# Head softmax ordered over pairs of blocks, its inverse from Ln and Exp with a Newton step, expert gates and ups in separate banks, and layer-norm roots as powers on POOL

## The chip, the core and the metric

The kernel runs on one core of a Trainium2 chip. The core has a matrix engine (TensorE, PE in the profile; its weight loads are the row PEld), a vector engine (VectorE, DVE), an engine for activation functions (ScalarE, ACT), a general engine (GpSimd, POOL), and an engine that issues transfers (SyncE, SP). Each works through its own instructions in order and waits on the others through semaphores. ScalarE holds one set of function tables at a time; a change of set appears in the profile as an instruction of its own, ACT_TABLE_LOAD. The metric is the time of one execution in device microseconds (us), the median of several runs.

## What is computed

Two batches of 1024 tokens of 128 features, all in 32-bit floats, pass through eight residual blocks: x = x + f(layernorm(x)) for each f. The first layer has a latent attention, a spiking feed-forward, a state-space block and the spiking feed-forward again. The second layer has a linear attention, an expert feed-forward, a head attention and the expert feed-forward again. The parts that matter here are the layer norm, the state space's softplus, the head attention and the experts:

```python
def _layernorm(x, axis=-1, eps=1e-05):
    m = jnp.mean(x, axis=axis, keepdims=True)
    v = jnp.var(x, axis=axis, keepdims=True)
    return (x - m) / jnp.sqrt(v + eps)
...
    dp = jnp.einsum('bhqd,bhkd->bhqk', q, k) * SCALE      # 16 heads of 8 features
    attn = jax.nn.softmax(dp, axis=1)                     # over the heads, not the keys
    w_avg = jnp.einsum('bhqk,bhkd->bhqd', attn, v)
...
    def expert_step(acc, w):                              # 8 experts, summed for every token
        wg, wu, wd = w
        h = jax.nn.silu(x @ wg) * (x @ wu)
        return (acc + h @ wd, None)
```

The head attention's softmax runs over the 16 heads: for each pair of a query and a key, the 16 exponentials are divided by their sum. The delta of the state space is softplus(...), which the kernel works out with an Exp and an Ln.

## The kernel before

Tokens lie 128 to a tile, so there are 16 tiles, 8 to a batch. The first layer and the linear attention, with a part of the first expert feed-forward beside them, take the trace up to about 1068 us. Then heads_and_experts (L1128) does the head attention of both batches together with most of both expert feed-forwards, and experts_ffn (L924) does the last four tiles' experts.

**Layer norms.** StagedNorm (L49) takes mean and variance on DVE (stats), a square root on ACT (root, L66), a reciprocal on DVE (L69), and, where ACT is to apply the norm, a shift of -mean/deviation on DVE (L77). The state space's double norm (L655 to L666) works out two variances with six small DVE operations and takes both square roots on ACT.

**Head attention.** For each batch, each query tile and each key tile there is one block: 128 keys by 128 queries by 16 heads, 128 blocks in all. A block passes these steps, each on its engine:

- products (L1231): PE writes the scores of 16 heads into PSUM, four banks, of which there is one set (ps_s);
- maxima (L1248) and the subtraction (L1254), each over 128x2048, on DVE;
- exponentials (L1257) on ACT, two instructions of 128x1024;
- lower (L1262): SP copies the exponentials of heads 0 to 7 into a buffer for a pair of blocks; upper (L1265): POOL issues a transfer that adds those of heads 8 to 15;
- denominators (L1271): PE sums the eight parts and turns them in the same go, into a bank h_pd of its own (one buffer, ps_d), both blocks of the pair, first half of the heads (end of an even iteration), then the second half (odd iteration);
- inverse (L1283): DVE's reciprocal over both blocks; turned (L1288): PE turns it back; evacuated (L1292): ACT copies it out of PSUM;
- normalize (L1296): POOL multiplies a block's 128x2048 exponentials with the inverse;
- weigh (L1301): PE applies the values, 32 narrow matmuls.

**Experts beside them.** An expert unit is 256 tokens (a chunk), one of 8 experts and one of 4 slices of its hidden features: 320 units here. In ExpertStream.products (L1051) a unit takes one PSUM bank (e_pgu, two buffers): Wg's product in one half, Wu's in the other. gates (L1067) applies Silu to the first half on ACT, multiply (L1075) multiplies with the second on DVE, outputs (L1085) adds Wd's product to a sum. Up to two units are started in each iteration; where PE has a side step instead (turning a finished chunk, a step of a norm or of a preparation), one.

**Order.** The order of the stage is written out by hand (manual_schedule): one loop over i (L1374 and on), in which every engine gets its instructions in the order of the text. Iteration i makes the scores of block i+1, its maxima, subtraction and exponentials, the summing transfer of block i, normalizes block i-4 and weighs block i-5. Even and odd iterations differ in the denominators and in the inverse, which is made at the start of an even one. The function aside gives one step of a side list to an engine where it fits: openings of expert chunks (L1030: statistics, root, shift, application, turning) and preparations of the next batch (L1168). Before and after the loop, alone (L1340) runs the experts without heads.

## Time and profile before

| | |
|---|---|
| time, median of 3 runs | 2212.57 us (2206.4 to 2213.07) |
| the profiled execution | 2201.0 us, of which the span of the trace is 2199.3 us |
| PE busy | 1876.8 us, 85% |
| DVE busy | 1656.2 us, 75% |
| ACT busy | 1324.5 us, 60% |
| POOL busy | 870.1 us, 40% |
| first and last scores of the head stage | 1184.8 and 2039.0 us |
| table loads of the head stage's gates and exponentials | 134 and 128, 1283 ns each |
| granted TensorE clock, mean | 0.943 |

Busy shares are means over the whole span, and the stages differ: a share says little of what a stage waits for. In a line of a group the columns are the kernel's line, the engine, the operation, the tiles written and read, their shapes and the number of instructions; then the busy time in us and the mean in ns; then the idle time of the engine just before them and what ended it. In a line of the timeline the first number is the start in us from the start of the span, the second the time that the merged instructions took, and a bracket gives the idle time before and its releaser.

### The profile page before, as it was taken

To read this page: it belongs to the slowest core of one execution; us is meant where nothing else is said; L and a number is where in the kernel's file an instruction comes from. 1 tells how busy PE (TensorE), PEld (TensorE's weight loads), DVE (VectorE), ACT (ScalarE), POOL (GpSimd) and SP (SyncE) were. 2 spreads that over 40 slices of the span, in tenths; PEclk is the share of its full clock that TensorE was granted. 3 is DMA by queue.
4 is the path that set the end of the run, shared out by engine and by line. 5 is a ranking of instruction groups with operands and counts; after the bars stand their busy time and mean duration, and the time that the engine had idled before them with its cause. 6 is when DMAs were issued, how large, how long until landed. Compare 5 with 4: busy or idle time off the path is not lost. (4 is left out here: it accounts for less than half of the span.)

```text
span 2199.3 us, 33893 instructions
## 1 busy us (share of the span) xinstructions
PE 1876.8 (85%) x13632; PEld 1068.8 (49%) x13632; DVE 1656.2 (75%) x1955; ACT 1324.5 (60%) x1762; POOL 870.1 (40%) x432
## 2 busy tenths in 40 slices
PE   7669888889967758898688899999888999998999
PEld 4223243333334323334455566666566666666754
DVE  5976867898774699894424989889888989998422
ACT  1026512276633666763544888888888888888422
POOL 0013400063401000000100778777877878887600
PEclk9989979979988979999899999999999999999999
DMA  4000000197623287530001656665655666666200
GB/s 91 1 1 1 1 1 0 49 228 165 157 71 99 57 201 174 136 82 0 1 1 48 154 153 159 155 161 148 160 152 155 165 154 159 168 159 154 68 5 5
DMA packets 73789, 220.01 MB, mean 100 GB/s; under 512 B 9184, under 2 KB 19872, under 8 KB 73504
## 3 DMA queue, kind: packets, MB, share of 16 engines
q1 hardware_dynamic: 54736, 149.40, 23.3%
q0 software_dynamic: 18432, 67.12, 16.0%
q8 instruction: 107, 1.75, 0.3%
q10 hardware_dynamic: 464, 1.33, 0.3%
q14 instruction: 50, 0.41, 0.1%
HBM read 78.35 MB, written 5.24 MB: 38 GB/s over the span
## 5 line engine op out<-in xcount | busy, mean ns | idle before, releaser
L1296 POOL TENSOR_TENSOR h_e<-h_e,h_r 128x2048 f32<-128x2048 f32 x128 | 599.8, 4687 | 109.6 <-issue 100.0
L1248 DVE TENSOR_REDUCE h_m<-h_s 128x128 f32<-128x2048 f32 x128 | 292.7, 2287 | 71.4 <-PE h_s L1237 71.4
L1254 DVE TENSOR_TENSOR h_e<-h_s,h_m 128x2048 f32<-128x2048 f32 x128 | 293.2, 2290 | 9.6 <-DVE h_m L1248 0.4
L1257 ACT ACTIVATE h_e<-h_e 128x1024 f32<-128x1024 f32 x256 | 256.5, 1049 | 23.0 <-DVE h_e L1254 19.4
L1067 ACT ACT_TABLE_LOAD x134 | 171.9, 1283 | 71.6 <-PE e_pgu L1060 70.5
L385 POOL TENSOR_SCALAR_AFFINE_SELECT a_pT<-a_pT 128x256 f32<-128x256 f32 x120 | 128.5, 1092 | 203.2 <-ACT a_pT L382 200.5
L1060 PE MATMUL e_pgu<-e_uT,Wg 128*128 128x256 f32 x640 | 199.8, 395 | 4.4 <-ACT h_qz L1204 2.3
L1075 DVE TENSOR_TENSOR e_h<-e_sg,e_pgu 128x256 f32<-128x256 f32 x320 | 119.6, 402 | 107.7 <-ACT e_sg L1067 103.9
L287 DVE TENSOR_REDUCE a_nm<-a_s 128x2 f32<-128x1024 f32 (+7 forms) x144 | 167.9, 1217 | 38.3 <-PE a_s L278 26.8
L1060 PE MATMUL e_pgu<-e_uT,Wu 128*128 128x256 f32 x640 | 193.8, 385 | 0.0
L1237 PE MATMUL h_s<-h_qz,h_kT 32*128 32x512 f32 x1024 | 153.5, 668 | 46.0 <-DVE h_e L1254 43.2
L1085 PE MATMUL h_po<-e_h,Wd 128*128 128x256 f32 x640 | 188.7, 412 | 4.0 <-DVE e_h L1075 2.3
L1271 PE MATMUL h_pd<-ident,h_e 128*128 128x128 f32 x1024 | 144.9, 279 | 40.8 <-DMA h_e<-h_e 40.7
L1265 POOL DMA_DIRECT2D h_e<-h_e x128 | 119.5, 933 | 140.8 <-DVE h_m L1248 67.7
L382 ACT ACTIVATE a_pT<-a_st 128x1024 f32<-128x1024 f32 (+3 forms) x176 | 129.9, 791 | 65.4 <-PE a_st L368 62.6
L1067 ACT ACTIVATE e_sg<-e_pgu 128x256 f32<-128x256 f32 x320 | 111.5, 382 | 91.6 <-PE e_pgu L1060 76.3
L1257 ACT ACT_TABLE_LOAD x128 | 164.2, 1283 | 2.3
L1085 PEld LDWEIGHTS h_po<-e_h,Wd 128*128 128x128 f32 x640 | 112.8, 196 | 105.6 <-issue 78.9
L800 DVE TENSOR_TENSOR_SCAN s_h<-s_a,s_h 128x1024 f32<-128x1024 f32 x64 | 148.7, 2323 | 17.9 <-ACT s_a L768 14.1
L269 PE MATMUL a_s<-a_latT,a_qT 32*128 32x512 f32 (+3 forms) x768 | 117.0, 583 | 42.0 <-DVE a_nm L287 40.0
L1271 PEld LDWEIGHTS h_pd<-ident,h_e 128*128 128x128 f32 x1024 | 116.7, 142 | 66.7 <-DMA h_e<-h_e 47.0
L1301 PE MATMUL h_po<-h_e,h_vz 128*32 128x128 f32 x4096 | 138.4, 276 | 7.3 <-DVE x_res L1398 6.1
(293 smaller groups left out, 3118.2 us busy)
## 6 DMA issues: line engine op xcount, KB each, us to landing
h_e<-h_e SPq DMA_DIRECT2D x128, 512.0 KB, 4.6
h_e<-h_e POOLq DMA_DIRECT2D x128, 512.0 KB, 5.4
s_a<-s_steps SPq DMA_DIRECT2D x64, 512.0 KB, 5.1
s_h<-s_steps SPq DMA_DIRECT2D x64, 512.0 KB, 6.5
s_steps<-s_gate SPq DMA_DIRECT2D x8, 256.0 KB, 2.0
Wg<-in_Wg_dram SPq DMA_DIRECT2D x8, 256.0 KB, 5.9
Wu<-in_Wu_dram SPq DMA_DIRECT2D x8, 256.0 KB, 5.9
Wd<-in_Wd_dram SPq DMA_DIRECT2D x8, 256.0 KB, 6.0
```

The costliest lines, as they stand in the source:

```text
L287: nc.vector.tensor_reduce(nm[:, half, i, h : h + together], s[:, :, :n], AX.X, ALU.max, negate=True)
L800: nc.vector.tensor_tensor_scan(h, a, h, 0.0, ALU.mult, ALU.add)
L1060: nc.tensor.matmul(pgu[:, k, :], w[name][:, e, f], uT, start=True, stop=True)
L1067: nc.scalar.activation(sg, pgu[:, 0, :], AF.Silu)
L1085: nc.tensor.matmul(self.sums, self.w["Wd"][:, e, fc, :], h, start=False, stop=last, skip_group_check=True)
L1237: nc.tensor.matmul(s[:, j, :].rearrange("p (k q) -> p k q", k=K), kTs[b][quad, bass.ts(kb, P)], qzs[b][qb // 4][quad, :, bass.ts(qb % 4, P ...
L1248: nc.vector.tensor_reduce(m, heads.rearrange("p h q -> p q h"), AX.X, ALU.max)
L1254: nc.vector.tensor_sub(e, heads, m.unsqueeze(1).to_broadcast([P, H, P]))
L1257: nc.scalar.activation(eh, eh, AF.Exp, scale=scale)
L1271: nc.tensor.matmul(pd[:, t, :], pair[:, t, k, :], g.ident, start=(k == 0 and t == 0), stop=(k == 7), is_transpose=True, skip_group_check=True,
L1296: nc.gpsimd.tensor_mul(e, e, r.unsqueeze(1).to_broadcast([P, H, P]))
L1301: nc.tensor.matmul(po[32 * j : 32 * j + 32, :], vz[:, kb * J + j, k].rearrange("p a d -> p (a d)"), a[:, 4 * j + k, :], start=False, stop= ...
```

## The change

Four things change.

- **Norms.** root becomes two POOL operations, an addition of epsilon and a power of -0.5; the square roots on ACT and the reciprocals on DVE go. The state norm's chain of six DVE operations and a square root becomes three POOL operations. In the loop the side step of a root moves from ACT's place to POOL's.
- **The inverse of the denominators.** The reciprocal on DVE is replaced by exp(-ln(d)) on ACT (seed), and a Newton step of two operations on DVE (refined). The sign that the step leaves is turned in the copy on ACT (evacuated). A one-column Ln of a constant (log_and_exp) is put behind the gates of each odd iteration.
- **The order.** The denominators are summed block by block of a pair, not half by half: the first block at the end of an even iteration, the second near the start of the odd one, followed there by the seed. The refinement, the turning and the copy stay in the even iteration.
- **The experts.** An odd iteration makes the gate products of up to two pairs of units, a bank for a pair (rise), and their Silus over 512 columns (open_gates). The even iteration makes the Wu products of the same pairs in banks of their own (follow_up). The next odd iteration multiplies (multiply_pairs). PE's side steps take the place of one of the two banks of an odd iteration, or stand in an even one if fewer than two pairs are open. The preparations of the next batch now also wait until the chunks that they read have been added.

```diff
         make_identity(nc, self.ident)
-        self.eps = self.const.tile([P, 1], F32, name="eps")
-        nc.vector.memset(self.eps, EPS)
+        self.power = self.const.tile([P, 1], F32, name="power")
+        nc.vector.memset(self.power, -0.5)
...
     def root(self):
-        self.g.nc.scalar.activation(self.rs, self.mv[:, :, 1], AF.Sqrt, bias=self.g.eps)
-
-    def inverse(self):
-        self.g.nc.vector.reciprocal(self.rs, self.rs)
-
-    def inverse_and_shift(self):
-
-
-        self.inverse()
-        self.shift = self.g.small.tile([P, self.nt], F32, name=f"{self.key}_nb", bufs=2)
+        g = self.g
+        g.nc.gpsimd.tensor_scalar(self.rs, self.mv[:, :, 1], EPS, None, ALU.add)
+        g.nc.gpsimd.tensor_tensor(self.rs, self.rs, g.power.to_broadcast([P, self.nt]), ALU.pow)
+
+    def shift(self):
+
+        self.nb = self.g.small.tile([P, self.nt], F32, name=f"{self.key}_nb", bufs=2)
         for t in range(self.nt):
             self.g.nc.vector.tensor_scalar(
-                self.shift[:, t : t + 1], self.mv[:, t, 0:1], self.rs[:, t : t + 1], -1.0, ALU.mult, ALU.mult
+                self.nb[:, t : t + 1], self.mv[:, t, 0:1], self.rs[:, t : t + 1], -1.0, ALU.mult, ALU.mult
             )
...
             self.g.nc.scalar.activation(
-                dst[:, t, :], self.src[:, t, :], AF.Identity, bias=self.shift[:, t : t + 1], scale=self.rs[:, t : t + 1]
+                dst[:, t, :], self.src[:, t, :], AF.Identity, bias=self.nb[:, t : t + 1], scale=self.rs[:, t : t + 1]
             )
...
         rs = g.small.tile([P, 2, 4], F32, name="s_rs", bufs=2)
-        nc.vector.tensor_scalar(rs[:, 0, :], mv[:, :, 1], EPS, None, ALU.add)
-        nc.vector.reciprocal(rs[:, 0, :], rs[:, 0, :])
-        nc.vector.tensor_mul(rs[:, 1, :], rs[:, 0, :], mv[:, :, 1])
-        nc.vector.tensor_scalar(rs[:, 1, :], rs[:, 1, :], EPS, None, ALU.add)
-        nc.vector.reciprocal(rs[:, 1, :], rs[:, 1, :])
-        nc.vector.tensor_mul(rs[:, 1, :], rs[:, 1, :], rs[:, 0, :])
-        nc.scalar.activation(rs, rs, AF.Sqrt)
+        nc.gpsimd.tensor_scalar(rs[:, 1, :], mv[:, :, 1], 1.0 + EPS, EPS * EPS, ALU.mult, ALU.add)
+        nc.gpsimd.tensor_scalar(rs[:, 0, :], mv[:, :, 1], EPS, None, ALU.add)
+        rf = rs.rearrange("p a b -> p (a b)")
+        nc.gpsimd.tensor_tensor(rf, rf, g.power.to_broadcast([P, 8]), ALU.pow)
         yield
...
         self.g, self.w, self.work, self.ps, self.sums, self.zero = g, w, work, ps, sums, zero
+        self.risen, self.opened, self.paired, self.added = [], [], [], set()
         self.units, self.fresh, self.gated, self.ready, self.summed, self.done = [], [], [], [], [], []
...
         yield "dve", lambda: ln.stats(range(2))
-        yield "act", ln.root
-        yield "dve", ln.inverse_and_shift
+        yield "pool", ln.root
+        yield "dve", ln.shift
         yield "act", lambda: ln.apply_on_act(u)
...
         nc = self.g.nc
-        for chunk, e, fc, pgu in self.fresh:
-            sg = self.work.tile([P, 2 * P], F32, name="e_sg", bufs=4)
-            nc.scalar.activation(sg, pgu[:, 0, :], AF.Silu)
-            self.gated.append((chunk, e, fc, pgu, sg))
+        if self.fresh:
+            two = self.work.tile([P, 2, 2 * P], F32, name="e_sg2")
+            for k, (chunk, e, fc, pgu) in enumerate(self.fresh):
+                nc.scalar.activation(two[:, k, :], pgu[:, 0, :], AF.Silu)
+                self.gated.append((chunk, e, fc, pgu, two[:, k, :]))
         self.fresh = []
...
         nc = self.g.nc
-        for chunk, e, fc, pgu, sg in self.gated:
-            h = self.work.tile([P, 2 * P], F32, name="e_h", bufs=4)
-            nc.vector.tensor_mul(h, sg, pgu[:, 1, :])
-            self.ready.append((chunk, e, fc, h))
+        if self.gated:
+            two = self.work.tile([P, 2, 2 * P], F32, name="e_h2")
+            for k, (chunk, e, fc, pgu, sg) in enumerate(self.gated):
+                nc.vector.tensor_mul(two[:, k, :], sg, pgu[:, 1, :])
+                self.ready.append((chunk, e, fc, two[:, k, :]))
         self.gated = []
+
+    def rise(self, banks):
+
+        for _ in range(banks):
+            pair, self.units = self.units[:2], self.units[2:]
+            if pair:
+                self.risen.append((pair, self.halves("Wg", pair)))
+
+    def halves(self, name, pair):
+        pgu = self.ps.tile([P, 4, P], F32, name="e_pgu").rearrange("p (k a) b -> p k (a b)", k=2)
+        for k, (chunk, e, fc, uT) in enumerate(pair):
+            self.g.nc.tensor.matmul(pgu[:, k, :], self.w[name][:, e, bass.ts(fc, P)], uT, start=True, stop=True)
+        return pgu
+
+    def open_gates(self):
+        for pair, pgu in self.risen:
+            sg = self.work.tile([P, 2, 2 * P], F32, name="e_sg2")
+            self.g.nc.scalar.activation(sg[:, : len(pair)], pgu[:, : len(pair)], AF.Silu)
+            self.opened.append((pair, sg))
+        self.risen = []
+
+    def follow_up(self):
+        self.paired += [(pair, sg, self.halves("Wu", pair)) for pair, sg in self.opened]
+        self.opened = []
+
+    def multiply_pairs(self):
+        for pair, sg, pgu in self.paired:
+            h = self.work.tile([P, 2, 2 * P], F32, name="e_h2")
+            self.g.nc.vector.tensor_mul(h[:, : len(pair)], sg[:, : len(pair)], pgu[:, : len(pair)])
+            self.ready += [(chunk, e, fc, h[:, k, :]) for k, (chunk, e, fc, uT) in enumerate(pair)]
+        self.paired = []
...
             self.turned = None
+            self.added.add(chunk)
             xt = self.tokens(chunk)
...
         nc.vector.memset(zero, 0.0)
+        ones = one.tile([P, 1], F32, name="h_ones")
+        nc.vector.memset(ones, 1.0)
+        spare = one.tile([P, 1], F32, name="h_spare")
         held = ps_o.tile([P, 4 * P], F32, name="h_po")
...
                 yield "dve", lambda t=t: ln.stats((t, t + 1))
-            yield "act", ln.root
-            yield "dve", ln.inverse_and_shift
+            yield "pool", ln.root
+            yield "dve", ln.shift
             yield "act", lambda: ln.apply_on_act(u)
...
-        def denominators(pd, pair, half):
-
-            for k in range(4 * half, 4 * half + 4):
-                for t in range(2):
-                    nc.tensor.matmul(
-                        pd[:, t, :],
-                        pair[:, t, k, :],
-                        g.ident,
-                        start=(k == 0 and t == 0),
-                        stop=(k == 7),
-                        is_transpose=True,
-                        skip_group_check=True,
-                    )
-
-        def inverse(pd):
-            rT = work.tile([P, 2, P], F32, name="h_rT")
-            nc.vector.reciprocal(rT, pd[:, 0:2, :])
+        def denominators(pd, pair, t):
+
+            for k in range(8):
+                nc.tensor.matmul(
+                    pd[:, t, :],
+                    pair[:, t, k, :],
+                    g.ident,
+                    start=(t == 0 and k == 0),
+                    stop=(k == 7),
+                    is_transpose=True,
+                    skip_group_check=True,
+                )
+
+        def seed(pd):
+            rT = work.tile([P, 2, P], F32, name="h_rT", bufs=1)
+            nc.scalar.activation(rT, pd[:, 0:2, :], AF.Ln)
+            nc.scalar.activation(rT, rT, AF.Exp, scale=-1.0)
             return rT
+
+        def refined(pd, rT):
+
+            t = work.tile([P, 2, P], F32, name="h_t", bufs=1)
+            nc.vector.tensor_mul(t, rT, pd[:, 0:2, :])
+            nc.vector.scalar_tensor_tensor(rT, t, 2.0, rT, ALU.subtract, ALU.mult)
...
             r = work.tile([P, 2, P], F32, name="h_r")
-            nc.scalar.copy(r, pd[:, 2:4, :])
+            nc.scalar.mul(r, pd[:, 2:4, :], -1.0)
             return r
+
+        def log_and_exp():
+            nc.scalar.activation(spare, ones, AF.Ln)
...
-        side = [(0, 28 if k else 16, ex.opening(c)) for k, c in enumerate(first[1:])]
-        side += [(0, 64, preparation(1, 0))]
-        side += [(2 * c + 2, 16 if c else 28, ex.opening(c)) for c in second]
-        side.insert(len(first) + 1, (0, 24, preparation(1, 1)))
+        side = [(0, 28 if k else 16, ex.opening(c), ()) for k, c in enumerate(first[1:])]
+        side += [(0, 64, preparation(1, 0), first[:2])]
+        side += [(2 * c + 2, 16 if c else 28, ex.opening(c), ()) for c in second]
+        side.insert(len(first) + 1, (0, 24, preparation(1, 1), first[2:]))
         finished, current, head, ex.unopened = 0, None, None, len(first)
...
                         if not side or side[0][0] > finished or len(ex.units) > side[0][1]:
+                            return False
+                        if not ex.added.issuperset(side[0][3]):
                             return False
...
             spread(0)
-            e_, pairs, d_, r_ = {}, {}, {}, {}
+            e_, pairs, d_, r_, s_ = {}, {}, {}, {}, {}
...
                 now, resting, oT = resting, oT, None
+                even = i % 2 == 0
                 if i + 1 < n:
                     heads = products(*blocks[i + 1])
-                even = i % 2 == 0
-                due = even and 0 <= i - 4 < n
-                if due:
-                    rT = inverse(d_[i - 4])
+                if not even:
+                    ex.multiply_pairs()
+                pair = i - 4 if even else i - 3
+                due = 0 <= pair < n
+                if due and even:
+                    refined(d_[pair], s_[pair])
+                    turned(d_[pair], s_.pop(pair))
+                    r_[pair] = evacuated(d_.pop(pair))
+                elif due:
+                    denominators(d_[pair], pairs.pop(pair), 1)
+                    s_[pair] = seed(d_[pair])
                 if now is not None:
...
                     ex.outputs()
-                ex.multiply()
-                if due:
-                    turned(d_[i - 4], rT)
-                    r_[i - 4] = evacuated(d_.pop(i - 4))
-                ex.products(1 if ex.turn() or aside("pe") else 2)
+                if not even:
+                    ex.rise(1 if ex.turn() or aside("pe") else 2)
+                else:
+                    if len(ex.opened) < 2 and not ex.turn():
+                        aside("pe")
+                    ex.follow_up()
                 if resting is not None:
...
                 aside("act")
-                ex.gates()
+                if not even:
+                    ex.open_gates()
+                    log_and_exp()
                 if i + 1 < n:
...
                 aside("dve")
-                pair = i - 2 if even else i - 3
-                if not even and 0 <= pair < n:
-                    denominators(d_[pair], pairs.pop(pair), 1)
                 if 0 <= i - 4 < n:
...
                 aside("pool")
+                if even and 0 <= i - 2 < n:
+                    d_[i - 2] = ps_d.tile([P, 4, P], F32, name="h_pd")
+                    denominators(d_[i - 2], pairs[i - 2], 0)
                 if 0 <= i - 5 < n:
...
-                if even and 0 <= pair < n:
-                    d_[pair] = ps_d.tile([P, 4, P], F32, name="h_pd")
-                    denominators(d_[pair], pairs[pair], 0)
+            ex.follow_up()
+            ex.multiply_pairs()
             while ex.busy() or side or current:
```

Left out are the places where inverse and inverse_and_shift are called in the first layer: the former call is dropped, the latter becomes shift.

More of the change, by code (lines that the diff above doesn't have):

```diff
@@ L232, in project @@
                 ln.root()
-                ln.inverse()
                 ln.apply(u, range(4), nc.vector)
@@ L541, in spiking_steps @@
         yield
-        ln.inverse()
         ln.apply(u, range(4), nc.vector)
@@ L845, in linear_steps @@
         yield
-        ln.inverse_and_shift()
+        ln.shift()
         ln.apply_on_act(dst)
@@ L949, in opening @@
         yield
-        ln.inverse_and_shift()
+        ln.shift()
         ln.apply_on_act(u)
```

## The prediction

> **What bounds the kernel now.** I read the page first, for the span and the heaviest groups, then the busy time of the head stage by itself, then one round of it in order of time on ScalarE, and last the only places of the trace where a logarithm and an exponential follow each other.
>
> ```profile
> span 2199.3 us, 33893 instructions
> L1296 POOL TENSOR_TENSOR h_e<-h_e,h_r 128x2048 f32<-128x2048 f32 x128 | 599.8, 4687 | 109.6 <-issue 100.0
> L1067 ACT ACT_TABLE_LOAD x134 | 171.9, 1283 | 71.6 <-PE e_pgu L1060 70.5
> L1257 ACT ACT_TABLE_LOAD x128 | 164.2, 1283 | 2.3
> ```
>
> From the page: each table load takes 1283 ns, and the head stage has one ahead of its gates (L1067) and one ahead of its exponentials (L1257), so two per block and four per pair of blocks.
>
> ```profile
> 1185.00:2043.00 858.00, 764.91 (x7502) 535.28 (x7502) 772.50 (x654) 729.04 (x915) 666.66 (x251) 0.98 0.61 156
> ```
>
> The stage's busy time (columns: stretch, length, then PE, PEld, DVE, ACT, POOL): 128 blocks in 858 us are 13.4 us per pair. DVE is busy 12.07 of it, PE 11.95, ACT 11.39, POOL 10.42. All are close; no engine has 3 us to spare per pair.
>
> ```profile
> 1455.69 2.29 DVE L1248 TENSOR_REDUCE h_m<-h_s 128x128 f32<-128x2048 f32 x1 [0.61 <-PE h_s L1237]
> 1460.28 1.75 DVE L1283 RECIPROCAL h_rT<-h_pd 128x256 f32<-128x256 f32 x1
> 1468.48 2.29 DVE L1248 TENSOR_REDUCE h_m<-h_s 128x128 f32<-128x2048 f32 x1 [0.61 <-PE h_s L1237]
> ...
> 1439.56 1.24 PE L1271 MATMUL h_pd<-ident,h_e 128*128 128x128 f32 x7 [2.00 <-DMA h_e<-h_e]
> ```
>
> The timeline: a quiet pair lasts 1468.48 - 1455.69 = 12.79 us, set by DVE (two maxima and two subtractions of 2.29, the reciprocal of 1.75, two pairs of gate products, and 0.6 of waiting for the scores). The other 0.6 us of the mean of 13.4 are stalls like the last line: PE waits for the summing DMA before it can turn the denominators.
>
> ```profile
> 454.34 1.28 ACT L716 ACT_TABLE_LOAD   x1
> 455.63 0.63 ACT L716 ACTIVATE s_xc<-s_xc 128x512 f32<-128x512 f32 x1
> 456.28 1.28 ACT L768 ACT_TABLE_LOAD   x1
> 457.58 1.15 ACT L768 ACTIVATE s_a<-s_a,s_negA 128x1024 f32<-128x1024 f32 x1
> ...
> 1709.51 0.37 ACT L1292 COPY h_r<-h_pd 128x256 f32<-128x256 f32 x1
> 1710.02 4.54 POOL L1296 TENSOR_TENSOR h_e<-h_e,h_r 128x2048 f32<-128x2048 f32 x1 [2.77 <-issue]
> ```
>
> This decides the case. L716 is the state space's Ln, L768 its Exp. The Ln needed a load after an Exp, and the next Exp needed one again: here Ln and Exp do not share a table. All eight Ln of the trace have their own load (L716, x8), and an Exp behind one loads again (L768, L382, L871).
>
> **The change, part by part.**
>
> *DVE in the head stage.* Per pair it loses the reciprocal, 1.75, and gains a product with a PSUM operand (like the gate product of 128x256, 0.40) and a scalar-tensor-tensor of 128x256 (half of L574's 0.72 for 128x512 plus start, 0.4): -0.95. Four gate products of 0.40 become two of 128x512 (L1214 has 0.69 for that): -0.2. Its quiet floor goes from 12.79 to about 11.6, or 12.2 because in the even iteration it then waits for the scores: the gap from a subtraction to the next maximum is at least 1.27 (PE needs 1.14), and only 0.8 fills it.
>
> *PE.* Same matmuls in another order; 11.95 busy stays.
>
> *Table loads on ACT.* In program order an odd iteration now issues seed Ln, seed Exp, the Silus, the one-column Ln (log_and_exp), the exponentials; an even one only the copy of the reciprocals and exponentials. With Ln and Exp in different tables as at 454 us, each of the five changes of function in the odd iteration is a load: 5 instead of 4 per pair, +1.283. The one-column Ln, put before the exponentials, costs a load and saves none. ACT besides: seed Ln like the PSUM copy of 128x256, 0.37; seed Exp like a gate of 128x256, 0.38; one-column Ln 0.21 (L666); Silus 4 x 0.382 to 2 x 0.597 (L966), about -0.31 at the 233 gates run in the stage; nine square roots with their loads leave the stage, 9 x (1.283+0.297)/64 = -0.22. ACT: 11.39+1.28+0.37+0.38+0.21-0.31-0.22 = 13.1 busy per pair, 13.4 with 15 to 20 gaps of 0.02. So ACT alone now needs what a pair takes today.
>
> The Trainium skill ("ScalarE: Activation LUTs", section on table sets) says that an Ln followed by an Exp costs one load, because one set has both; by that rule the pair would have two loads instead of five. The trace contradicts it at 454 to 458 us, and I go by the trace. "ScalarE activation tables" (section on the compiler and the runtime) says that loads are placed for the longest run, which would also have picked the shared set; the same two loads speak against it. By these rules the sum would be that of the first rival below.
>
> *New waits, and the round they make.* ACT's round, from the end of the even exponentials: load 1.28, seed Ln 0.37, load 1.28, seed Exp 0.38, load 1.28, Silus 1.19, load 1.28, Ln 0.21, load 1.28, odd Exps 2.0, copy 0.37, even Exps 2.0: 12.9, and 0.47 of side work. Three things wait on it or hold it.
> (a) ps_d has one buffer. In an even iteration the next pair's first denominators (PE) now stand ahead of the weighing and must wait for the copy of the inverse; that copy stands on ACT behind the odd exponentials and their load. Behind the waiting matmuls PE has, in order, the weighing, the next scores, the second block's denominators, and for the last of these ACT's seed Ln waits. This is a closed round: copy 0.37, hand-over 0.3 (1300.66 shows 0.29 from the copy to the next denominators), denominators 0.96, weighing 1.08, scores 1.14, denominators 0.96, hand-over 0.2, then on ACT Ln, load, Exp, load, Silus, load, Ln, load, Exps: 9.27. Sum 14.3, with ten gaps of 0.02 and some 0.2 of side work **14.7 us**. The even exponentials run beside PE's part. If the Ln's own load also stands behind its wait, 1.28 more: **16.0**. The trace has both: L1067's load waits with its Silu for PE (71.6 idle before it), while at L686 the load ran at 316.74 and only the Silu, at 330.25, waited 12.23 for PE. No row is nearer, so I take the middle, 15.3, and keep 14.7 and 16.0 as ends; below, if the copy's place did not bind at all, ACT's 13.1 is left.
> (b) The seed Ln waits with that for the summing DMA. Behind it stand the Silus (Wu on PE), the odd exponentials (SP's lower copy, POOL's sum) and the copy (POOL's multiply). From the copy to the second sum issued after it POOL takes 9.9 (1696.20 to 1706.06), landing 5.5, turn 1.0, hand-overs 0.3: 16.7, and ACT 9.6 from the Ln to the copy, 26.3 over two rounds; two rounds of 15.3 are 30.6, so the late transfers of now, 0.2 to 2.3 each, are covered. At two rounds of 13.1 they would not be.
> (c) The refinement on DVE waits for the seed; behind it stand maxima and subtraction. ACT has the seed 6.7 after the copy, DVE is free for it at 8.1 (3.5 to the end of the scores, 4.6 for both passes): covered by 1.4.
> Loop: 64 pairs x (15.3 - 13.4) = **+122 us** (-19 for 13.1, +83 for 14.7, +166 for 16.0).
>
> *Expert units.* A pass that spends PE's side slot gave up one of two units; now in an odd iteration it gives up one bank of two units, and an even slot is free only after that. Of 256 units the stage ran 233. Eight preparation steps come in a row and cost 8 as before; seven openings and seven turns cost 14 before and up to 28 now. 0 to 14 units more stay for the tail, where two take 2.6 us (1067's rows at 2098.31 and 2100.90): 0 to +18, taken **+9**, as some will meet. SP and POOL issue the same DMAs. SP's lower copy leaves with the odd exponentials and lands 4.7 later; POOL's sum on it stands behind the even multiply, 0.37 + 0.14 + 4.7 = 5.2 after the same exponentials: covered by 0.5.
>
> *Inverse roots on POOL.* 29 StagedNorms and 4 state norms: Sqrt 0.30 plus reciprocal 0.17 become two POOL operations; 27 loads go. No row shows a power. Nearest: POOL copy of 128x32 0.21 and memset 0.10 below, product of 128x512 1.27 above; so a norm costs -0.3 to +1.0 against the old. I take about 0.5 for the two, near the small rows, as 2 to 8 elements a partition are worked on. Loads that truly stood in the way are few: DVE waited for the old root 2.4 (h), 2.1 (l), 1.2 (e), 0.7 (f) and 0.8 (a, ex). The state norm's six DVE operations of 0.17 save 4 us of an engine with 0.81 busy in 290 to 640 us. In the loop POOL stands behind a multiply of 4.7, and nine shifts on DVE may wait up to 1 us each. Together **-4 us** (-10 to +10). If POOL were later than its consumer everywhere, 33 norms would pay 1 us each; the yields between root and use cover that.
>
> **Sum.** 122 + 9 - 4 = +127. The profiled execution took 2201.0 us (span 2199.3, 1.7 around it): 2328. The runs shown have a median of 2212.6, 11.6 above it: 2340 on that base. I say 2334, between.
>
> **Rivals.** *Ln and Exp share a table* (the change ends faster): one load serves seed, exponentials and one-column Ln, so 2 per pair. The round in (a) loses two of its four loads, 14.7 - 2.57 = 12.1, ACT falls to 9.5, and DVE's 12.2 plus half of today's stalls bounds: 12.5, 64 x -0.9 = -58, with +9 - 4: -53, 2154. It decides at two loads per pair; at three the round, 13.4, is what a pair takes today. For it: no Ln of the trace comes right behind a Silu, as the one-column Ln does, so that order is not shown. Against it: every Ln that the trace has.
> *The copy does not hold PE* (another buffer, or the turn done in time), and ACT runs at its busy 13.1 to 13.4: loop -19 to 0, with the rest 2193 to 2212 around 2207, no change to tell. For it: today PE waited for the copy twice only, 0.6 in all. Against it: today the copy follows DVE's reciprocal, not ten instructions of ACT with five loads.
> *The load waits, and POOL's powers take over 1 us in 33 norms*: 166 + 18 + 10: 2401.
>
> **How the numbers follow.** ACT's round as in (a) 0.80; no hold 0.06; shared table 0.09; the worst 0.05. 0.3% of 2207 is 6.6 us, about what a measurement here tells from none. Faster: 0.09 and a third of the no-hold case, 0.11. Same: 0.03. Slower: 0.86. The range is that of the first case, from 14.7 with the tail at nothing and the norms at -10 (2207 + 83 - 10 = 2280, less 5 for my durations) to 16.0 with the tail at 18 and the norms at 10 (2401); with one case holding 0.80 the others stay outside.
>
> **What would show it.** Right: about 5 loads per pair, on the lines of the seed's Ln, the seed's Exp, Silu, log_and_exp and the exponentials; PE idle for the copy ahead of the denominators by 1 us or more per pair; ACT idle ahead of the seed's Ln for 1 to 3 us; DVE idle for PE's scores far above 0.6 per pair; no Sqrt left. Wrong: no load on the seed's Exp or the exponentials; ACT below 75%, DVE still bound; or PE waiting for DMA as now with ACT idle behind it.

## The result and the profile after

The changed kernel takes 2275.5 us (median of 4 runs, 2271.0 to 2278.6). The kernel before, run beside it on the same chip, took 2212.1 us. The ratio is 1.0291, with a 95% interval of 1.0266 to 1.0315: 63 us slower. The profiled execution took 2275.3 us, close to its median; that of before, 2201.0 us, lies 11 us under its own, so two traces set side by side show 74 us where the medians show 63.

Where the 74 us of the traces lie follows from the rows of the scores (h_s). The first scores start at 1183.1 us (1184.8 before), the last at 2094.0 (2039.0): the head stage's loop lasts 910.9 us instead of 854.2, +56.7. From the last scores to the end it is 179.4 instead of 160.3, +19.1. The time ahead of the loop is 1.7 shorter.

The page's groups and the groups of table loads of the changed kernel (after the bars: busy us and mean ns, then idle time before them). Here and below, only the lines of a view that the text reads are shown:

```profile
span 2273.4 us, 33995 instructions
L1278 DVE TENSOR_REDUCE h_m<-h_s 128x128 f32<-128x2048 f32 x128 | 292.5, 2285 | 104.7 <-PE h_s L1267 104.5
...
L1332 ACT ACT_TABLE_LOAD x68 | 87.2, 1283 | 1.2
L1090 ACT ACT_TABLE_LOAD x67 | 86.0, 1283 | 1.2
L1287 ACT ACT_TABLE_LOAD x64 | 82.1, 1283 | 1.1
L1313 ACT ACT_TABLE_LOAD x64 | 82.1, 1283 | 1.2
L1312 ACT ACT_TABLE_LOAD x63 | 80.8, 1283 | 1.1
```

Each pair of blocks has five loads: the one-column Ln of log_and_exp (L1332), Silu (L1090), the exponentials (L1287), the seed's Exp (L1313) and the seed's Ln (L1312). The loads themselves waited for nothing, 1.1 us in 63: they ran ahead of the waits of their instructions. The one-column Ln, put there for the exponentials, has a load of its own, and the exponentials behind it load again.

The busy time of the loop (columns: stretch, length, then PE, PEld, DVE, ACT, POOL):

```profile
1185.00:2097.00 912.00, 741.02 (x7434) 520.81 (x7433) 789.39 (x583) 827.41 (x1016) 674.07 (x268) 0.98 0.57 146
```

ACT is busy 827 of 912 us, 91%, or 12.9 per pair. It is now the busiest engine, but it is not full. A quiet pair lasts 13.9 us: from one copy of the inverse (L1328) to the next it is 1451.51 - 1437.58 = 13.93. The round after it is 14.57 long, with 0.63 us of side work in it (two copies, L1473 and L1474). That round of ACT in order of time:

```profile
1437.58 0.36 ACT L1328 ACTIVATE h_r<-h_pd 128x256 f32<-128x256 f32 x1
...
1451.51 0.36 ACT L1328 ACTIVATE h_r<-h_pd 128x256 f32<-128x256 f32 x1
1452.95 2.00 ACT L1287 ACTIVATE h_e<-h_e 128x1024 f32<-128x1024 f32 x2 [1.08 <-DVE h_e L1284]
...
1455.53 1.28 ACT L1312 ACT_TABLE_LOAD   x1
1456.83 0.39 ACT L1312 ACTIVATE h_rT<-h_pd 128x256 f32<-128x256 f32 x1
1457.23 1.28 ACT L1313 ACT_TABLE_LOAD   x1
...
1464.16 2.00 ACT L1287 ACTIVATE h_e<-h_e 128x1024 f32<-128x1024 f32 x2
1466.08 0.36 ACT L1328 ACTIVATE h_r<-h_pd 128x256 f32<-128x256 f32 x1
1466.88 2.00 ACT L1287 ACTIVATE h_e<-h_e 128x1024 f32<-128x1024 f32 x2 [0.44 <-DVE h_e L1284]
1468.90 1.28 ACT L1312 ACT_TABLE_LOAD   x1
```

ACT's only gap between these two copies is ahead of the even exponentials, 1.08 us, and DVE ends it. Why DVE is late shows on DVE, POOL and PE around it:

```profile
1446.27 2.06 DVE L1320 SCALAR_TENSOR_TENSOR h_rT<-h_t,h_rT 128x256 f32<-128x256 f32 x1
1448.26 2.28 DVE L1278 TENSOR_REDUCE h_m<-h_s 128x128 f32<-128x2048 f32 x1
1460.20 2.04 DVE L1320 SCALAR_TENSOR_TENSOR h_rT<-h_t,h_rT 128x256 f32<-128x256 f32 x1
...
1443.18 4.86 POOL L1335 TENSOR_TENSOR h_e<-h_e,h_r 128x2048 f32<-128x2048 f32 x1
1457.15 4.81 POOL L1335 TENSOR_TENSOR h_e<-h_e,h_r 128x2048 f32<-128x2048 f32 x1
...
1448.39 0.44 PE L1324 MATMUL h_pd<-ident,h_rT 128*128 128x128 f32 x2 [1.19 <-DVE h_rT L1320]
1451.93 1.09 PE L1300 MATMUL h_pd<-ident,h_e 128*128 128x128 f32 x8 [0.51 <-ACT h_r L1328]
```

Two things meet here. The second operation of the Newton step (L1320) takes 2.06 and 2.04 us, though its fastest in the stage takes 0.42. It ends at 1448.33 and 1462.24, 0.3 us after POOL's multiplies (1448.04 and 1461.96). And PE's first denominators (L1300) wait for ACT's copy, as predicted. Over 1300 to 2050 us the waits on these paths are:

```profile
PEld h_pd L1324 <- DVE h_rT L1320: 97.9, 52, 3.3
DVE h_m L1278 <- PE h_s L1267: 85.6, 54, 4.6
PE h_pd L1300 <- ACT h_r L1328: 61.6, 50, 3.6
ACT h_e L1287 <- DVE h_e L1284: 37.8, 44, 2.6
```

(Total us, times, the longest.) Two closed rounds can be followed in the rows, and both come to 13.9. The first is the prediction's (a): copy, first denominators, weighing, scores, second denominators, the seed, the gates, the odd exponentials, copy (1437.58 to 1451.51). The second goes over two pairs: copy at 1451.51, denominators, weighing, scores, maximum and subtraction, the Newton step with its stretched operation (end 1462.24), the next maximum and subtraction, the even exponentials at 1466.88, the load at 1468.90, and from there to the copy 10.55 more, as from 1455.53 to 1466.08, where the seed's Ln waits for nothing: 27.9, twice 13.95. (This time the Ln waited 0.54 us more for PE, and the copy came at 1479.98.) The traces alone don't say which one sets the pace.

### The profile page after: what moved, and what is told of

The parts are those of the page before. It is cut to its first block, busy times and chain, and to the rows that moved or that the text cites. A ratio compares the mean times of both kernels' runs of the same rounds, so it can differ in the third digit from the quotient of the medians.

```text
span 2273.4 us, 33995 instructions
## 1 busy us (share of the span) xinstructions
PE 1871.5 (82%) x13632; PEld 1068.3 (47%) x13632; DVE 1673.1 (74%) x1843; ACT 1400.7 (62%) x1834; POOL 919.8 (40%) x510
## 5 line engine op out<-in xcount | busy, mean ns | idle before, releaser
L1284 DVE TENSOR_TENSOR h_e<-h_s,h_m 128x2048 f32<-128x2048 f32 x128 | 293.1, 2290 | 9.1 <-issue 0.4
L1287 ACT ACTIVATE h_e<-h_e 128x1024 f32<-128x1024 f32 x256 | 256.4, 1049 | 47.4 <-DVE h_e L1284 46.3
L1300 PE MATMUL h_pd<-ident,h_e 128*128 128x128 f32 x1024 | 143.8, 285 | 75.1 <-ACT h_r L1328 75.1
L1300 PEld LDWEIGHTS h_pd<-ident,h_e 128*128 128x128 f32 x1024 | 113.5, 144 | 149.4 <-ACT h_r L1328 98.9
L1111 PE MATMUL h_po<-e_h,Wd 128*128 128x256 f32 x640 | 175.4, 394 | 4.1 <-DVE e_h L1070 1.6
L1295 POOL DMA_DIRECT2D h_e<-h_e x128 | 131.3, 1026 | 52.3 <-DVE h_e L1284 43.3
L958 ACT ACTIVATE e_sg<-e_pg 128x512 f32<-128x512 f32 x96 | 57.3, 597 | 131.1 <-PE e_pg L955 108.8
L355 PE MATMUL a_st<-a_qT,a_latT 32*128 32x512 f32 (+3 forms) x768 | 120.4, 561 | 10.4 <-ACT a_pT L378 8.2
L963 DVE TENSOR_TENSOR e_h<-e_sg,e_pu 128x512 f32<-128x512 f32 x96 | 64.6, 684 | 83.9 <-PE e_pu L956 71.8
L1340 PEld LDWEIGHTS h_po<-h_e,h_vz 128*32 128x32 f32 x4096 | 106.7, 111 | 35.7 <-issue 32.8
L956 PE MATMUL e_pu<-e_uT,Wu 128*128 128x512 f32 x192 | 102.7, 617 | 19.3 <-DVE e_h L963 19.3
L1084 PE MATMUL e_pgu<-e_uT,Wu 128*128 128x256 f32 x480 | 117.7, 386 | 0.1
```

Of the source, the lines that this page charges most:

```text
L1111: nc.tensor.matmul(self.sums, self.w["Wd"][:, e, fc, :], h, start=False, stop=last, skip_group_check=True)
L1284: nc.vector.tensor_sub(e, heads, m.unsqueeze(1).to_broadcast([P, H, P]))
L1287: nc.scalar.activation(eh, eh, AF.Exp, scale=scale)
L1295: nc.gpsimd.dma_start(out=e2, in_=e[:, 8:16, :], accum_op=ALU.add)
L1300: nc.tensor.matmul(pd[:, t, :], pair[:, t, k, :], g.ident, start=(t == 0 and k == 0), stop=(k == 7), is_transpose=True, skip_group_check=True,
L1340: nc.tensor.matmul(po[32 * j : 32 * j + 32, :], vz[:, kb * J + j, k].rearrange("p a d -> p (a d)"), a[:, 4 * j + k, :], start=False, stop= ...
```

## The experiments

Each was run beside the kernel before on its own chip (2208 to 2213 us there); a ratio is to that, with its 95% interval. Not all runs had the same chip, so a few us between two of them say little. None leaves out a part of the reference's computation.

**One load less.** The one-column Ln is left out.

```diff
                     ex.open_gates()
-                    log_and_exp()
```

> The one-column Ln behind the gates is left out, so the exponentials load their table straight from the Silu's: four loads per pair in place of five. Theory A (ACT's round of loads, closed through the copy of the inverse, the next denominators, weighing and scores, sets the pace at 13.9 us per quiet pair): the round is shorter by 1.28 + 0.20 = 1.5, a quiet pair is 12.4 to 13.2, the time 2275 - 64 x (0.7 to 1.5) = 2180 to 2231. Theory B (the Newton step's second operation on DVE, 1.99 us at the median where 0.42 is its shortest, sets the pace): DVE's work is untouched, 2265 to 2276. Theory C (the new order alone is slow, whatever ACT does): 2270 to 2276.

Measured: 2215.4 us, ratio 1.002 (1.000 to 1.004), 60 us less than the changed kernel, 0.94 per pair. Four loads a pair are left: L1090 x65 and L1284, L1309, L1310 x64. So the loads are on the path. Of the 1.5 us a pair of ACT's work taken away (load 1.28, Ln 0.20) more than a third did not come out, and the Newton step's second operation was still stretched, 1.92 us in the median.

**Ln and Exp from one set.** In place of the one-column Ln, an explicit load of the table set that holds both.

```diff
         def log_and_exp():
-            nc.scalar.activation(spare, ones, AF.Ln)
+            nc.scalar.preload_act_table_set("natural_log_exp_and_others")
```

> In place of the one-column Ln stands an explicit load of the table set that holds both Ln and Exp; seed and exponentials then find their functions there, so two loads per pair are left in place of five. Theory A: the round loses 3 x 1.28 + 0.2 = 4.0, so something else bounds: DVE with the stretched step, 12.8 to 13.3 per pair; time 2275 - 64 x 1.1 = 2205, 2180 to 2225, level with the kernel before. If the stretch too came from waiting on ACT, 2155 (the first rival of the prediction). Theory B: 2260 to 2276. Theory C: 2265 to 2276.

Measured: 2156.3 us, ratio 0.974 (0.971 to 0.977). This version is faster than both kernels. Its groups of loads in the stage, and the operation on DVE (least, median and greatest ns):

```profile
L1329 ACT ACT_TABLE_LOAD x68 | 87.2, 1283 | 1.2
L1090 ACT ACT_TABLE_LOAD x67 | 86.0, 1283 | 1.9 <-DVE e_h L1101 0.7
...
L1317 DVE SCALAR_TENSOR_TENSOR h_rT<-h_t,h_rT x56: 390/1128/4753, 1305.6 to 1992.9; 128x256 f32<-128x256 f32 x56
```

Two loads a pair, none at the seed or the exponentials: the set that was loaded by name serves Ln and Exp in turn. ACT falls to 72% and now waits for DVE's subtraction (158 us of 700); DVE is at 93%. The three loads that the changed kernel has more, with the one-column Ln, cost 2275.5 - 2156.3 = 119 us. That is more than the 50 to 95 us that were expected while DVE's operation stays stretched: it is still stretched, but less (1.13 us in the median instead of 1.99).

**Both denominators late.** They are made in the odd iteration, behind the scores, so that PE has the next scores before it waits for the copy.

```diff
                 elif due:
-                    denominators(d_[pair], pairs.pop(pair), 1)
+                    d_[pair] = ps_d.tile([P, 4, P], F32, name="h_pd")
+                    for t in range(2):
+                        denominators(d_[pair], pairs[pair], t)
+                    pairs.pop(pair)
...
-                if even and 0 <= i - 2 < n:
-                    d_[i - 2] = ps_d.tile([P, 4, P], F32, name="h_pd")
-                    denominators(d_[i - 2], pairs[i - 2], 0)
```

> Both halves of the denominators are made in the odd iteration, behind its scores, so nothing on PE waits for the copy of the inverse any more except the denominators themselves; five loads stay. Theory A: the closed round opens, ACT's own 13.1 to 13.4 per pair is left: 2275 - 64 x (0.5 to 0.9) = 2218 to 2243, PE's wait for the copy gone. If ACT's queue alone sets the pace and the hold by the copy is only a symptom: 2265 to 2276, with ACT over 95% busy. Theory B: 2265 to 2280.

Measured: 2277.9 us, ratio 1.030 (1.026 to 1.033): nothing gained. The denominators' wait for the copy is gone from the waits, and still a quiet pair takes 13.9 us. The timeline of DVE:

```profile
1439.23 2.29 DVE L1284 TENSOR_TENSOR h_e<-h_s,h_m 128x2048 f32<-128x2048 f32 x1
1441.88 2.90 DVE L1320 SCALAR_TENSOR_TENSOR h_rT<-h_t,h_rT 128x256 f32<-128x256 f32 x1
1453.09 2.29 DVE L1284 TENSOR_TENSOR h_e<-h_s,h_m 128x2048 f32<-128x2048 f32 x1
1455.88 2.94 DVE L1320 SCALAR_TENSOR_TENSOR h_rT<-h_t,h_rT 128x256 f32<-128x256 f32 x1
```

1453.09 - 1439.23 = 13.86. The stretched operation got longer, 2.65 us in the median instead of 1.99. Taken alone this run says that the hold of PE is a symptom; the next two show that this is too simple.

**The Newton product in PSUM.** The product stays in the free half of the denominators' bank, so that the second operation reads one operand from PSUM and one from SBUF.

```diff
-            t = work.tile([P, 2, P], F32, name="h_t", bufs=1)
+            t = pd[:, 2:4, :]
             nc.vector.tensor_mul(t, rT, pd[:, 0:2, :])
             nc.vector.scalar_tensor_tensor(rT, t, 2.0, rT, ALU.subtract, ALU.mult)
```

> The Newton step's product goes to the free half of the denominators' PSUM bank, so that its second operation reads one operand from PSUM and one from SBUF; nothing else changes. If the stretch comes from two SBUF operands beside POOL's multiply, that operation falls from 1.99 at the median to about 0.4. Theory A: the round through the copy still takes 13.9, a change of -15 to 0: 2260 to 2276. Theory B: DVE's chain is shorter by 1.4 per pair, over two pairs 0.7 to 0.8 each: 2220 to 2235. If the stretch stays, 2270 to 2280, and its cause is another.

Measured: 2271.6 us, ratio 1.027 (1.024 to 1.031): 4 us less than the changed kernel, with intervals that overlap. The operation, the seed's Ln in two rounds, PE's denominators behind the copy, and the wait for it:

```profile
L1320 DVE SCALAR_TENSOR_TENSOR h_rT<-h_pd,h_rT x48: 423/423/426, 1313.2 to 1992.7; 128x256 f32<-128x256 f32 x48
...
1443.41 0.38 ACT L1312 ACTIVATE h_rT<-h_pd 128x256 f32<-128x256 f32 x1 [0.86 <-PE h_pd L1300]
1457.32 0.38 ACT L1312 ACTIVATE h_rT<-h_pd 128x256 f32<-128x256 f32 x1
...
1453.08 1.09 PE L1300 MATMUL h_pd<-ident,h_e 128*128 128x128 f32 x8 [1.74 <-ACT h_r L1328]
...
PE h_pd L1300 <- ACT h_r L1328: 105.4, 49, 4.0
```

The stretch is gone to the last instruction, and DVE's work with it; PE's wait for the copy has taken its place, 105.4 us of 700 against 57.8 in the changed kernel. This is round (a) alone: the seed's Ln ends its wait for PE at 1443.41 and 13.91 us later, at 1457.32, it runs again.

**Both.** The last two edits together, with all five loads.

> The changed kernel with both small repairs together: the denominators of both blocks late in the odd iteration, and the Newton step's product left in PSUM, so that DVE's second operation no longer has two SBUF operands. The five table loads stay. Theory A, from the two runs that opened one place each and moved nothing (2277.9 and 2271.6): there are two closed rounds of nearly the same length, ACT's copy to PE's denominators and DVE's stretched operation to ACT's exponentials, and each hides the other. With both open only ACT's own work is left, 12.9 us of instructions a pair in the quiet part of the run with the product in PSUM, 13.2 to 13.4 with gaps and side work: the loop loses 58 to 70 us of 911, total 2205 to 2240. Rival B, something third holds the pace (the transfers, or the exponentials waiting on the scores): 2258 to 2276.

Measured: 2228.6 us, ratio 1.008 (1.005 to 1.012). Alone, the two edits moved the time by +2 and -4 us, neither clear of noise; together they take 47 off it. There were two rounds of the same length, and each hid the other. ACT's rows now follow each other without a gap:

```profile
1448.59 2.00 ACT L1287 ACTIVATE h_e<-h_e 128x1024 f32<-128x1024 f32 x2
1450.61 1.28 ACT L1312 ACT_TABLE_LOAD   x1
1461.42 1.99 ACT L1287 ACTIVATE h_e<-h_e 128x1024 f32<-128x1024 f32 x2
1463.43 1.28 ACT L1312 ACT_TABLE_LOAD   x1
```

A pair takes 1463.43 - 1450.61 = 12.82 us of ACT's own work, 13.6 in the mean over the loop (869.3 us), where PE waits for the summing transfer again (14.2 us of 650).

**Shared set and product in PSUM.** The edits of the second and fourth run together.

> The changed kernel with one load of the table set that holds Ln and Exp (two loads a pair), and the Newton product in PSUM. Theory A: with two loads DVE sets the pace, and the stretch of its second Newton operation (1.13 us median against 0.42) is part of it: 0.7 to 0.9 a pair goes, less what the scores then keep DVE waiting: 2110 to 2140 against 2156. Rival B, DVE merely waits as much longer for the scores: 2148 to 2162. No load but the two per pair in either case.

Measured: 2138.3 us, ratio 0.968 (0.964 to 0.971): 18 us less than with the shared set alone (14 by the ratios, as the two ran on different chips), near the upper end of what was expected. The timeline of DVE, which sets the pace here:

```profile
1438.44 2.29 DVE L1275 TENSOR_REDUCE h_m<-h_s 128x128 f32<-128x2048 f32 x1
1443.48 0.42 DVE L1317 SCALAR_TENSOR_TENSOR h_rT<-h_pd,h_rT 128x256 f32<-128x256 f32 x1
1444.45 2.29 DVE L1275 TENSOR_REDUCE h_m<-h_s 128x128 f32<-128x2048 f32 x1 [0.55 <-PE h_s L1264]
1450.39 2.29 DVE L1275 TENSOR_REDUCE h_m<-h_s 128x128 f32<-128x2048 f32 x1
```

A quiet pair is 11.95 us, of which 0.55 is a wait for the scores; the loop's mean is 12.2 (779.8 us).

**The same with late denominators.**

> As the last, and the denominators of both blocks late in the odd iteration. With the shared set the hold of PE by the copy is already small (0.2 us a pair), so theory A says no gain: within 10 us of the last, and rather above it, as ACT's seed then waits longer for PE. Rival B, PE's order still holds the scores back: 15 us or more below the last.

Measured: 2170.2 us, ratio 0.982 (0.978 to 0.985): 32 us more. That is neither of the two expectations, though the first had the sign. ACT's seed waits 62.2 us of 650 for PE (21.7 without the edit), and the maxima wait 68.1 us for the scores (41.1). With two loads the first denominators are better early, where they do not wait for the copy.

**The norms alone.** The kernel before with only its inverse roots as powers on POOL (the hunks of root, shift and the state norm in the diff).

> The kernel before with one part of the change alone: all inverse roots as powers on POOL. The prediction put this part at -4 us (-10 to +10): 2202 to 2222. From the trace after, an addition and a power for four columns take 0.24 and 1.04 us, against 0.30 and 0.17 before and a load of 1.28 less where one was in the way; the linear attention ended 6 us later there. Theory A: 2205 to 2220, with the loss ahead of the head stage. Rival B, powers behind POOL's long multiplies delay the head stage by their own: 2228 or more.

Measured: 2199.1 us, ratio 0.996 (0.994 to 0.998): 9 us less, a little better than the first expectation, and with no net loss ahead of the head stage. The powers in its trace, for 2, 4 and 8 columns, and who waited:

```profile
L68 POOL TENSOR_TENSOR ex_rs<-ex_rs,power x10: 713/718/719, 1080.3 to 1994.9; 128x2 f32<-128x2 f32 x10
L68 POOL TENSOR_TENSOR h_rs<-h_rs,power x4: 1037/1039/1042, 1089.0 to 1503.0; 128x4 f32<-128x4 f32 x4
L68 POOL TENSOR_TENSOR l_rs<-l_rs,power x4: 1663/1663/1664, 734.7 to 1052.7; 128x8 f32<-128x8 f32 x4
...
  DVE l_nb L74: 8.5, 4
```

The linear attention's last addition starts 6.3 us later (1074.1 against 1067.8), and the first scores all the same 1.4 earlier: the stretch between them is 7.7 shorter, with 10 us less of ACT's work in it. The loop is 3.0 shorter. The two traces differ by 4.5 us in all, half of what the medians show. That the loads of the square roots, gone there, make these gains fits the rows; no run took them apart.

**The order alone.** The changed kernel with the reciprocal on DVE in place of the Newton step, and no Ln at all.

```diff
         def seed(pd):
-            nc.scalar.activation(rT, pd[:, 0:2, :], AF.Ln)
-            nc.scalar.activation(rT, rT, AF.Exp, scale=-1.0)
...
         def refined(pd, rT):
-            nc.vector.tensor_mul(t, rT, pd[:, 0:2, :])
-            nc.vector.scalar_tensor_tensor(rT, t, 2.0, rT, ALU.subtract, ALU.mult)
+            nc.vector.reciprocal(rT, pd[:, 0:2, :])
...
-            nc.scalar.mul(r, pd[:, 2:4, :], -1.0)
+            nc.scalar.copy(r, pd[:, 2:4, :])
...
-                    log_and_exp()
```

> The changed kernel with the old way to the inverse: DVE's reciprocal of the denominators stands where the Newton step stood, the seed's Ln and Exp and the one-column Ln are gone, the copy out of PSUM keeps its sign. The order over two blocks, the gates and ups apart and the norms on POOL stay. ACT then changes tables twice a pair (Silu, then the exponentials). Theory A: order and gates apart cost nothing themselves, the whole loss is in the table loads of the Newton seed; DVE then has 4 x 2.29 + 1.28 + 1.75 = 12.2 us a pair and waits about as long for the scores as with the shared set: 12.3 to 12.9 a pair, 787 to 826 for the loop against 911, total 2148 to 2190. Rival B, the order itself (the first denominators behind the copy, the refinement's place on DVE) costs too: 2205 or more.

Measured: 2159.3 us, ratio 0.975 (0.972 to 0.978). Two loads a pair (L1284 x64, L1090 x64), loop 798.1 us or 12.5 per pair. The order over two blocks and the gates apart are a gain, not a loss. With the norms they take 54 us off the kernel before, of which the norms alone took 9. That the gain comes from the loads, which are half as many, fits; no run took the order and the gates apart. The Newton inverse as it was written puts 116 us on top.

**The linear attention's norms back on ACT,** in the fastest version.

```diff
     def root(self):
+        if self.key == "l":
+            g.nc.scalar.activation(self.rs, self.mv[:, :, 1], AF.Sqrt, bias=g.eps)
+            return
...
     def shift(self):
+        if self.key == "l":
+            self.g.nc.vector.reciprocal(self.rs, self.rs)
```

> The kernel with the shared set and the Newton product in PSUM (2138.3), with one more thing undone: the four norms of the linear attention take their root on ACT and their reciprocal on DVE again, as before the change; the other norms stay powers on POOL. In the trace of the norms alone the linear attention's last addition starts at 1074.1 instead of 1067.8. Theory A: those 6 us are on the path: 5 to 7 us less, 2130 to 2134. Rival B: the time up to the first scores is set by other work and takes the 6 us back: 2135 to 2142.

Measured: 2137.3 us, ratio 0.965 (0.961 to 0.968), 1 us under the run without the edit, with intervals that overlap. In the traces the last addition comes 5.5 us earlier and the first scores 5.7 (1172.9 against 1178.6), so those microseconds do reach the head stage, against the second expectation's reason; but the loop of this trace is 6.0 longer, and the time is what that expectation said. Whether the longer loop is chance or has a cause stays open.

## Why the prediction was right and wrong

The direction was right and the reason behind it too; the size was twice too large: +127 on its base, against +63. The time lies at the lower edge of the range (2275.5 us against 2275), and that it lies inside is partly luck. The loop's term came out at +57, below the lowest value that this edge was worked out from (+83). The stretch behind the last scores, 19 us longer where the edge took the tail at nothing, and the time ahead of the loop, 2 us shorter where it took 10 off for the norms, made up for it.

- **Table loads: right.** Five a pair, on the five lines named. The one-column Ln costs a load and saves none; leaving it out gives 60 us back. The Trainium skill ("ScalarE: Activation LUTs", section "Table sets: the hidden batching unit") has Ln and Exp in one set with one load. The runs show that set: it serves both once it is loaded by name (two loads a pair, 2156.3), but an Ln left to itself was not given it (2275.5 and 2215.4). So the count was right, but "Ln and Exp do not share a table" says too much: a set that serves both can be loaded, and here it was not the one that was.
- **Round (a): the mechanism right, the size wrong.** This is the term that was mis-sized. It was taken as 15.3 (14.7 to 16.0), and measures 13.9 where it stands alone. Of the 1.4 too much, 0.6 is the load of the seed's Ln, put half behind the wait as a middle: it ran ahead of the wait (idle before it 1.1 us in 63), so nothing was to be added. The rest is in the sum itself. From the Ln to the copy it had 9.27, and the rows, with the gaps between them, give 9.24 (1457.32 to 1466.56 with the product in PSUM); the 0.4 that was added for gaps and side work has no place in this round. From the end of the copy to the Ln it had 4.6, and the rows give 4.3 (1453.02 to 1457.32): the hand-over from the copy is 0.06 us (1453.02 to 1453.08), not 0.3. The loop's mean of 14.2 is 0.3 above the quiet pair, for which the sum had nothing, so the term comes out at 64 x 0.9 = +57 in place of +122.
- **"If the copy's place did not bind, ACT's 13.1 is left": wrong as it stood.** With the place moved alone nothing changed, because of the next point. With that removed as well it holds: 12.8 in a quiet pair, 13.6 in the mean.
- **The Newton step on DVE at 0.4 per operation, covered by 1.4 us: wrong.** The first operation, with a PSUM operand, takes 0.41. The second has two SBUF operands and takes 1.99 in the median, up to 4.5, beside POOL's multiply. The price came from the row of L574, whose first operand (f_py) lies in PSUM; the run with the product in PSUM has just that price, 0.42. And the cover was worked out for the seed's arrival, not for the operation's end. It did not add to the total, since round (a) was as long; it made a second bound that hid the first.
- **(b), the summing transfers covered: right.** PE's wait for them, 32.4 us between 1300 and 2000 us before, is gone. It comes back where the round gets shorter.
- **Expert units, +9: right for the tail, but the ramp-down was missed.** 28 units are left behind the last heads' addition instead of 21; seven at 1.3 us are 9, and that part is 11 longer (133 against 122). The other 8 lie between the last scores and that addition (46.4 us against 38.4), where the last head rounds run out. ACT has 14 table loads there instead of 3, DVE waits 9.0 us for the seed's Exp, and one Newton operation takes 4.49 us. No run took these apart.
- **Norms, -4 (-10 to +10): -9 when run alone, and priced wrongly on the way.** For four columns the power takes 1.04 and the addition 0.24, 1.3 together against 0.5 taken. There were also more norms than counted: 33 with a StagedNorm and 4 of the state space, 37 in place of 33. That the sum still came out near must come from larger gains as well; no run took them apart.
- **The shared-table rival** was worked out at 2154 and 12.5 a pair. With the set loaded by name it measures 2156.3 and 12.45. Its condition was not met by the code, and that the time fits so well is partly luck: DVE bounds, as it said, but with a Newton operation of 1.13 us that it took at 0.4. With that operation at 0.42 the kernel takes 2138.3 and 12.2.

The signs named in advance held for the loads, the wait of PE for the copy (57.8 us in 49 pairs, 1.2 each) and the maxima's wait for the scores. The seed's Ln was expected to stand idle for 1 to 3 us; it waited 17.9 us in 48 rounds, 0.4 each, since ACT came as late as PE.

## What to carry to other kernels

Count the table loads in the trace, not the functions in the code: here Ln and Exp, which one set can serve, loaded in turn until that set was loaded by name, and a dummy activation put there to choose it only added a load. When an edit that takes away the longest wait moves nothing, look for a second closed round of the same length and open both before calling the first a symptom. Test the parts of a change one by one: here the order and the norms gained 54 us, the inverse lost 116, and two lines (the set by name, the product in PSUM) turn the whole into 70 us gained.

## What the runs showed of the hardware

- In the changed kernel, a scalar-tensor-tensor of 128x256 on DVE with both operands in SBUF took 0.42 to 4.5 us, and where it was long it ended 0.3 us after POOL's 128x2048 multiply: behind the last scores it ran from 2106.54 to 2111.03 and the multiply from 2105.93 to 2110.74. One that started after the multiply's end (at 1579.36, the multiply ended at 1578.87) took 0.42. With one operand in PSUM all 48 took 423 to 426 ns. The Trainium skill ("SBUF — State Buffer", section "SBUF: two separate sides") calls the port pair that DVE and GpSimd share an exclusive lock, which a DVE instruction with two SBUF inputs takes against a GpSimd instruction that reads SBUF, the later one waiting for the whole of the earlier; these rows agree, with the operation's end 0.3 us behind the multiply's.
- A power on POOL took 0.72, 1.04 and 1.66 us for 2, 4 and 8 columns: a line through the three has 0.40 and 0.16 per column.
- The load of a table ran ahead of its instruction's wait at the seed's Ln (idle 1.1 us before 63 loads), and 0.01 to 0.02 us lay between a load and the activation behind it. At the gates of the kernel before, the load itself stood behind the wait (idle 71.6 us before 134 loads); no run shows on what this depends.
